# Two transformer layers on one core: the second layer's value products in pairs

## The chip, the core and the metric

The kernel runs on one core of one Trainium2 chip. The metric is device time in microseconds of one execution. The core has the engines that the profile names PE (TensorE, the matrix engine; PEld are its weight loads), DVE (VectorE), ACT (ScalarE), POOL (GpSimd) and SP (SyncE, which here only issues transfers). They work beside each other and wait for one another by semaphores; each takes its instructions in the order in which the program wrote them.

## The reference

The input `x` has 4 batches of 1024 tokens with 128 features, all in float32. Four blocks follow each other, each added to `x` after a layer norm:

```python
x = x + _layernorm(_L0_attn_ref(_layernorm(x), L0_attn_Wqkv, L0_attn_Wout))
x = x + _layernorm(_L0_ffn_ref(_layernorm(x), ...))      # attention and mixture of experts
x = x + _layernorm(_L1_attn_ref(_layernorm(x), L1_attn_w_qkv))
x = x + _layernorm(_L1_ffn_ref(_layernorm(x), U1, V1, b1, U2, V2, b2))
```

Three of these hold a causal attention with 16 heads:

```python
att = jnp.einsum('bhqd,bhkd->bhqk', q, k) * scale     # scores
att = jnp.where(causal, att, -jnp.inf)
att = jax.nn.softmax(att, axis=-1)
out = jnp.einsum('bhqk,bhkd->bhqd', att, v)           # value products
```

In the first and third attention a head has 8 features; the first clips its scores to plus and minus 10. The second attention, inside `_L0_ffn_ref`, takes keys and values from a latent of 16 features that all heads share, with rotary positions on part of the key; a mixture of 8 experts, two for each token, and a shared expert follow it.

## The kernel before

The kernel calls the three attentions its three layers: the classes `First`, `Second` and `Third`. A layer has 4 batches, and each batch 4 units of 4 heads: 48 units in all, numbers 0 to 15, 16 to 31 and 32 to 47. Within a unit there are two blocks of 512 queries (`h` is 0 or 1), and within a block a loop over key tiles of 128 tokens (`kt`): 4 tiles for `h` = 0, 8 for `h` = 1, because the rest is masked out. So a unit has 12 steps, and a layer 192. From tile 4h on a tile crosses the diagonal (the diagonal tiles): only the queries from `q0` on are computed, 512, 384, 256 and 128 of them.

**One step of the second and third layer.** For each of two pairs of heads (`pp` 0 and 1):

- `scores`: two matmuls of keys by queries into `ps_k`, for two heads beside each other in TensorE's rows. The second layer has 64 rows for each head (the profile writes 64\*128), the third 32 (32\*128).
- `weigh`: ACT takes the exponential of the two score tiles into a tile `pt`; on a diagonal tile POOL then masks the corner with an affine select (line 1257). `pt` has six buffers.
- `max_step`: two matmuls of scores the other way round, into `ps_q`, and their row maxima by DVE, for a unit about one unit ahead. The exponentials of both layers need these maxima beforehand: they are written as extra rows of the operands (`strips`), over a transpose (`ps_n`), a copy on ACT (`nT`) and a transfer issued by SP.

The scores of these two layers, the maxima and most other work share a ring of seven PSUM banks; the sum of the value products, `av`, has a bank of its own. Each float32 matmul shows as two instructions, which stream the operand twice.

**The value products.** `products` multiplies one key tile's weights `pt` by the values of four heads: four matmuls beside each other in TensorE's columns (128\*32, eight instructions), added up in `av` over the block's tiles. Two of the four read the `pt` of `pp` 0, and two that of `pp` 1. With a block's last tile `av` is copied to `num` by ACT, and the transposes to tokens (`ps_a`) are put among the other work for one step later.

The products of a tile are not written in the tile's own step. At the end of a step the tile is appended to `waiting`, and `next_products(keep)` takes the oldest entry if more than `keep` are there. It is called at these places:

- first layer and the very last unit: after both pairs' scores, with `keep` = 1;
- second layer (`u.width == R`): after both pairs, with `keep` = 0;
- third layer: between the two pairs, after `max_step` of the first one, with `keep` = 0.

So `waiting` also carries entries over from block to block and from layer to layer.

**Other work.** At the end of each step `other_work` writes pieces of projections, preparations and tails: the second layer's tail holds the experts (`pgu`, `pc`, `py`), the third layer's tail the feed-forward with its activation on 512-wide tiles (`ph` on TensorE, `sq` and `xb` on ACT, lines 1010 and 1011 on POOL). A planner in Python, at build time, chooses the pieces by due times and by an account of the work that TensorE, ACT and DVE still owe (`Metered`, `behind`); value products count in TensorE's account. All matmuls, ACT and DVE operations are recorded in a helper, so they all have line 96, and the profile is read by the names of the tiles.

Of the kernel before, what the change touches and what calls it, by code (L numbers as in the profile page):

```python
# [121 lines left out]
def sandwich(ctx: ExitStack, tc: tile.TileContext, a: dict, out: bass.AP):  # L122
# [20 lines left out]
    def mtile(name):  # L143
        return ring[0].tile([P, 512], F32, tag="s", name=name) if ring else ps_spare.tile([P, 512], F32, tag="m", name=name)
# [371 lines left out]
    def to_tokens(num, dst, width, ps, n=4):  # L516

        for i in range(n):
            nc.tensor.transpose(ps[:, i * P : (i + 1) * P], num[:, i * P : (i + 1) * P], ident)
        ps4 = ps[:, 0 : n * P].rearrange("p (i j r) -> p i j r", i=n, j=4)  # L520
        rec = pool2.tile([P, 4, 4], F32, tag="rec3", name="rec3")[:, 0:n]
        nc.vector.reciprocal(rec, ps4[:, :, :, width])
        nc.vector.tensor_tensor(
            dst.rearrange("p i (j d) -> p i j d", j=4), ps4[:, :, :, 0:width],
            rec.unsqueeze(3).to_broadcast([P, n, 4, width]), ALU.mult,
        )
# [605 lines left out]
    def need_free(k):  # L1132

        while not stages[k].att_free:
            behind[0][1].look(step_now[0])
            behind[0][1].piece(step_now[0])
            if behind[0][1].done:
                behind.popleft()

    def need_prep(n):  # L1140
        for i in range(n + 1):
            if not prep[i].done:
                need_input(i // NG)
                prep[i].finish()
# [19 lines left out]
    def max_step(n, h, qt, c, pp, mx, last):  # L1164
        u, g = units[n]
        need_prep(n)
        if h not in mx:
            mx[h] = pool2.tile([P, 4, 2, 2, h + 1], F32, tag=f"mx{h}", name="mx")
        w = min(512, (qt + 1) * P - 512 * c)
        ps = rtile("ps_q")  # L1170
        for jj in range(2):
            q, k = u.rows(g, pp, jj)
            nc.tensor.matmul(
                ps[jj][:, 0:w], lhsT=q[:, qt * P : (qt + 1) * P], rhs=k[:, 512 * c : 512 * c + w], start=True, stop=True
            )
        for jj in range(2):
            scores, to = ps[jj][:, 0:w], mx[h][:, qt - 4 * h, pp, jj, c : c + 1]
            if c == h:

                nc.vector.tensor_tensor_reduce(  # L1180
                    scores, scores, cmask[:, 512 - w : 512], 1.0, -3.0e38, ALU.add, ALU.max, to
                )
            else:
                nc.vector.tensor_reduce(to, scores, AX.X, ALU.max)
        if last:
            negated[n, h] = Task(u.negate(g, h, mx[h]))
            urgent.append(negated[n, h])

    def after(task, gen):
        yield LIGHT, 2  # L1190
        task.finish()
        yield from gen

    def products(n, h, kt, state, pts, q0):

        u, g = units[n]
        last = 4 * h + 3
        if kt == 0:
            state["acc"] = ps_av.tile([P, 512], F32, tag="av", name="av")
        acc = state["acc"]  # L1200
        for j in range(4):
            nc.tensor.matmul(
                acc[32 * j : 32 * j + 32, q0:512], lhsT=u.values(g, kt, j), rhs=pts[j // 2][:, j % 2, q0:512],
                start=kt == 0, stop=kt == last, tile_position=(0, 32 * j),
            )
        if kt == last:
            num = pool2.tile([P, 512], F32, tag="num", name="num")
            if n == len(units) - 1:

                for i in range(2):  # L1210
                    half = slice(256 * i, 256 * i + 256)
                    nc.scalar.copy(num[:, half], acc[:, half])
                    quarters.append(Task(u.quarter(num, 2 * h + i), 26))
                return
            nc.scalar.copy(num, acc)

            def back():
                yield SPARE, 2
                to_tokens(num, u.result(g, h), u.width, mtile("ps_a"))

            k = n // NG
            if g == 0 and h == 0 and k > 0:
                if u.width == R or stages[k - 1].width == R:
                    need_free(k - 1)
                elif k > 1:
                    need_free(k - 2)
            urgent.append(Task(back()))
            if g == NG - 1 and h == 1:
                tails[k] = Task(after(urgent[-1], u.tail()), u.pieces[1])
                behind.append((24 * NG * (k + 2) - 6, tails[k]))  # L1230

    def scores(n, h, kt, pps):

        u, g = units[n]
        q0 = max(0, kt * P - 512 * h)
        tiles = [rtile("ps_k") if ring else two_banks("ps_k") for pp in pps]
        for pp, ps in zip(pps, tiles):
            for jj in range(2):
                q, k = u.rows(g, pp, jj)
                nc.tensor.matmul(  # L1240
                    (ps[jj] if ring else ps[:, jj])[:, q0:512], lhsT=k[:, kt * P : (kt + 1) * P], rhs=q[:, 512 * h + q0 : 512 * h + 512],
                    start=True, stop=True,
                )
        return tiles, q0

    def weigh(n, h, kt, ps, q0):
        u, g = units[n]
        pt = pool6.tile([P, 2, 512], F32, tag="pt", name="pt")
        if ring:
            for jj in range(2):  # L1250
                nc.scalar.activation(pt[:, jj, q0:512], ps[jj][:, q0:512], AF.Exp, scale=u.scale)
        else:
            nc.scalar.activation(pt[:, :, q0:512], ps[:, :, q0:512], AF.Exp, scale=u.scale)
        u.clip(pt[:, :, q0:512])
        if kt >= 4 * h:

            nc.gpsimd.affine_select(  # L1257
                out=pt[:, :, q0 : q0 + P], in_=pt[:, :, q0 : q0 + P], compare_op=ALU.is_ge, fill=0.0, base=0,
                pattern=[[0, 2], [1, P]], channel_multiplier=-1,
            )  # L1260
        return pt
# [31 lines left out]
    def other_work(at, light=4):  # L1293

        taken = set()
        nc.pass_step()
        while t := pick(at, taken):
            if t.kind == LIGHT:
                light -= 1
                if not light:  # L1300
                    taken.add(LIGHT)
            else:
                taken.add(t.kind)
            t.piece(at)
# [7 lines left out]
    waiting = deque()  # L1312

    def next_products(keep):
        if len(waiting) > keep:
            products(*waiting.popleft())

    at = 0
    for n, (u, g) in enumerate(units):
        if n == B * NG:  # L1320
            first_banks.close()
            ring.append(ctx.enter_context(tc.tile_pool(name="ps_one", bufs=7, space=PSUM)))
        need_prep(n)
        for h in range(2):
            if n == 0 and h == 1:
                u.second.finish()
            if u.has_max and not negated[n, h].done:
                negated[n, h].finish()
            state = {}
            for kt in range(4 * h + 4):  # L1330
                if not u.has_max or n == len(units) - 1:

                    (a0, a1), q0 = scores(n, h, kt, (0, 1))
                    pts = [weigh(n, h, kt, ps, q0) for ps in (a0, a1)]
                    next_products(1)
                    for _ in range(2):
                        at += 1
                        if maxima and maxima[0][0] <= at:
                            max_step(*maxima.popleft()[1])
                else:  # L1340
                    pts = []
                    for pp in range(2):
                        (ps,), q0 = scores(n, h, kt, (pp,))
                        pts.append(weigh(n, h, kt, ps, q0))
                        at += 1
                        if maxima and maxima[0][0] <= at:
                            max_step(*maxima.popleft()[1])
                        if pp == 0 and u.width != R:
                            next_products(0)
                    if u.width == R:  # L1350
                        next_products(0)
                other_work(at)
                waiting.append((n, h, kt, state, pts, q0))
    while waiting:
# [53 lines left out]
```

## Time and profile before

| what | value |
|---|---|
| runs | 2198.24, 2201.5 and 2203.89 us, median 2201.5 |
| profiled execution, from first to last instruction | 2195.8 us |
| TensorE busy | 2102.2 us, 96% |
| DVE, ACT, POOL busy | 66%, 58%, 28% |
| scores `ps_k`, second layer (64\*128) | 1536 instructions, 335.9 us |
| value products `av`, second layer | 1536 instructions, 163.7 us |
| value products `av`, first and third layer | 3072 instructions, 336.9 us |
| masks on the diagonal, POOL line 1257 | 768 instructions, mean 445 ns |

The profiled execution has no time of its own beside its span: 2195.8 us is what its instructions cover, and the runs' median stands 5.7 us above that. Starts are counted from the span's first instruction. In the rows of the timeline an arrow in brackets names what ended the idle time before an instruction; the length of a matmul includes a modelled end, so two matmuls in a row overlap on paper. In a table by stages the columns are the stretch, its length, the busy time of PE, PEld, DVE, ACT and POOL with the number of instructions, the granted share of TensorE's clock, the DMA share and GB/s.

### The profile page before, as it was taken

How to read it: one execution, taken by the hardware profiler on the slowest of the kernel's cores; microseconds unless marked ns; L12 is line 12 of the kernel's file. 1: busy time of each engine (PE TensorE's matmuls, PEld its weight loads, DVE VectorE, ACT ScalarE, POOL GpSimd, SP SyncE). 2: the span in 40 equal slices, each digit the busy share in tenths (PEclk: the TensorE clock that was granted, in tenths of full speed). 3: DMA queues.
4: the chain of work that ended last, by engine and by line, in shares of the span. 5: the costliest groups of instructions: out<-in, count | busy, mean ns of one | idle time of the engine just before them, and what ended most of it. 6: DMA issues, size and time to landing. Idle time of an engine off the chain costs nothing.

```text
span 2195.8 us, 40904 instructions
## 1 busy us (share of the span) xinstructions
PE 2102.2 (96%) x14480; PEld 907.0 (41%) x14480; DVE 1444.6 (66%) x4265; ACT 1279.8 (58%) x2680; POOL 621.6 (28%) x1032
## 2 busy tenths in 40 slices
PE   7999999989999999999999999999999999999994
PEld 2333333324444444444444544343444444444432
DVE  5666666577656675567566675567668677677755
ACT  3676767744555554455445544455556766766776
POOL 3342323432233222223222211221122233322332
PEclk9999999999999999999999999999999999999996
DMA  2310000111111101111020100000000000000000
GB/s 58 66 17 11 11 11 11 26 39 26 26 39 31 26 16 35 26 26 26 6 54 18 26 9 6 7 7 6 7 7 7 12 7 17 12 7 16 7 1 20
DMA packets 32253, 42.98 MB, mean 20 GB/s; under 512 B 11553, under 2 KB 23841, under 8 KB 32049
## 3 DMA queue, kind: packets, MB, share of 16 engines
q1 hardware_dynamic: 31440, 40.04, 8.4%
q8 instruction: 115, 1.88, 0.4%
q14 instruction: 90, 0.73, 0.1%
q10 hardware_dynamic: 608, 0.33, 0.1%
HBM read 5.74 MB, written 2.10 MB: 4 GB/s over the span
## 4 chain that ended last, share of the span: by engine, by line
PE 83%; ACT 6%; DVE 6%; POOL 2%; issue 2%; DMA 0%; SPq 0%; ACTq 0%; POOLq 0%; DVEq 0%
PE ps_k L96 29%; PE ps_q L96 18%; PE av L96 18%; PE pgu L96 3%; ACT pt L96 3%; PE ps_a L96 2%; PE py L96 2%; PE pa L96 2%; DVE pt L96 1%; PE ps_t L96 1%; PE ps_p L96 1%; PE ps_o L96 1%; PE ps_v L96 1%; DVE ps_q L96 1%; PE ps_l L96 1%
## 5 line engine op out<-in xcount | busy, mean ns | idle before, releaser
L96 ACT ACTIVATE pt<-ps_k 128x512 f32<-128x512 f32 (+5 forms) x1920 | 952.0, 555 | 640.3 <-PE ps_k L96 440.8
L1257 POOL TENSOR_SCALAR_AFFINE_SELECT pt<-pt 128x256 f32<-128x256 f32 x768 | 333.5, 445 | 1173.0 <-ACT pt L96 864.7
L96 DVE CUSTOM_DVE_ANT_0 ps_q<-ps_q,cmask 128x256 f32<-128x256 f32 (+3 forms) x1024 | 481.1, 515 | 213.1 <-PE ps_q L96 204.9
L96 PE MATMUL ps_k<-strips 32*128 32x512 f32 (+3 forms) x3072 | 573.0, 538 | 9.7 <-ACT pt L96 2.4
L96 DVE TENSOR_REDUCE mx<-ps_q 128x1 f32<-128x512 f32 x512 | 328.7, 684 | 153.8 <-PE ps_q L96 152.3
L96 PE MATMUL ps_q<-strips 32*128 32x512 f32 (+3 forms) x1536 | 423.9, 537 | 6.0 <-ACT pt L96 3.5
L96 PE MATMUL av<-pt,vals 128*32 128x512 f32 (+3 forms) x3072 | 336.9, 502 | 25.3 <-ACT num L96 11.2
L96 PE MATMUL ps_k<-strips,kT 64*128 64x512 f32 (+3 forms) x1536 | 335.9, 511 | 1.2 <-ACT nT L96 1.2
L96 PEld LDWEIGHTS ps_k<-strips 32*128 32x128 f32 x3072 | 213.5, 186 | 285.4 <-ACT pt L96 105.6
L96 PE MATMUL ps_q<-kT,strips 64*128 64x512 f32 (+3 forms) x1536 | 323.1, 489 | 0.9 <-ACT pt L96 0.6
L96 DVE TENSOR_SCALAR pt<-pt 128x1024 f32<-128x1024 f32 (+3 forms) x384 | 227.1, 607 | 133.9 <-ACT pt L96 129.0
L96 PEld LDWEIGHTS ps_q<-kT,strips 64*128 64x128 f32 x1536 | 152.6, 188 | 117.6 <-issue 69.4
L96 PEld LDWEIGHTS ps_q<-strips 32*128 32x128 f32 x1536 | 164.3, 185 | 73.1 <-ACT pt L96 44.9
L96 PEld LDWEIGHTS ps_k<-strips,kT 64*128 64x128 f32 x1536 | 130.7, 186 | 150.6 <-issue 65.3
L96 PEld LDWEIGHTS av<-pt,vals 128*32 128x32 f32 x3072 | 63.6, 109 | 244.0 <-issue 106.8
L96 PE MATMUL av<-pt,v2l 128*32 128x512 f32 (+3 forms) x1536 | 163.7, 498 | 0.0
L96 DVE DVE_READ_ACCUMULATOR2_ANT mx<- 128x1 f32 x1024 | 144.5, 141 | 0.0
L384 POOL TENSOR_TENSOR rs<-rs,minus_half 128x8 f32<-128x8 f32 (+1 forms) x38 | 62.4, 1643 | 251.3 <-DVE rs L96 250.8
L96 PEld LDWEIGHTS av<-pt,v2l 128*32 128x32 f32 x1536 | 30.3, 108 | 104.6 <-issue 61.8
L96 PEld LDWEIGHTS ps_a<-ident,num 128*128 128x128 f32 x384 | 40.2, 140 | 72.3 <-issue 52.5
L96 PE MATMUL ps_a<-ident,num 128*128 128x128 f32 x384 | 63.3, 287 | 0.4 <-ACT num L96 0.4
L96 ACT COPY num<-av 128x512 f32<-128x512 f32 (+1 forms) x98 | 57.1, 586 | 10.5 <-PE av L96 10.1
(278 smaller groups left out, 1628.2 us busy)
## 6 DMA issues: line engine op xcount, KB each, us to landing
swapped<-rb SPq DMA_DIRECT2D x32, 256.0 KB
strips<-rp SPq DMA_DIRECT2D x64, 128.0 KB
strips<-packed SPq DMA_DIRECT2D x248, 32.0 KB
strips<-lat SPq DMA_DIRECT2D x64, 64.0 KB
strips<-nT SPq DMA_DIRECT2D x256, 1.0 KB
strips<-nT SPq DMA_DIRECT2D x128, 2.0 KB
x<-in_L_attn_x_dram SPq DMA_DIRECT2D x3, 512.0 KB
out_dram<-x SPq DMA_DIRECT2D x3, 512.0 KB
```

Of the source, the lines that this page charges most:

```text
L96: return call(*args, **kw)
L384: nc.gpsimd.tensor_tensor(rs[:, t], rs[:, t], minus_half[:, t], ALU.pow)
L1257: nc.gpsimd.affine_select(out=pt[:, :, q0 : q0 + P], in_=pt[:, :, q0 : q0 + P], compare_op=ALU.is_ge, fill=0.0, base=0, pattern=[[0, 2], [ ...
```

## The change

In the second layer the products are no longer written in each step. `paired_products` writes them when two tiles of the block wait, or when the oldest waiting tile belongs to another block than the current one, and then `next_products(0)` is to take all that wait. For this the `if` in `next_products` becomes a `while`. The other calls of `next_products` are left as they are.

```diff
     def next_products(keep):
-        if len(waiting) > keep:
+        while len(waiting) > keep:
             products(*waiting.popleft())
+
+    def paired_products(n, h):
+        if len(waiting) == 2 or waiting and waiting[0][:2] != (n, h):
+            next_products(0)
...
                         if pp == 0 and u.width != R:
                             next_products(0)
                     if u.width == R:
-                        next_products(0)
+                        paired_products(n, h)
                 other_work(at)
                 waiting.append((n, h, kt, state, pts, q0))
```

## The prediction, made before the changed kernel ran

> **What bounds the kernel now.** I read the page first, then the busy time by stage, then TensorE's timeline inside the second and the third layer.
>
> ```profile
> PE 2102.2 (96%) x14480; PEld 907.0 (41%) x14480; DVE 1444.6 (66%) x4265; ACT 1279.8 (58%) x2680; POOL 621.6 (28%) x1032
> PE 83%; ACT 6%; DVE 6%; POOL 2%; issue 2%; DMA 0%; SPq 0%; ACTq 0%; POOLq 0%; DVEq 0%
> ```
>
> TensorE is busy for 96% of the span, and the chain that ended last runs through it for 83%. The stretches below are the second layer (its first value products start at 528 us) and the third (from 1443 us).
>
> ```profile
> 528.00:1443.00 915.00, 911.97 (x5625) 424.10 (x5624) 575.35 (x1743) 463.34 (x1057) 227.88 (x352) 1.00 0.10 23
> 1443.00:2149.00 706.00, 690.24 (x5128) 293.50 (x5128) 497.16 (x1635) 459.46 (x1083) 194.69 (x332) 0.99 0.05 8
> ```
>
> After the stretch come PE, PEld, DVE, ACT and POOL busy time and the granted clock. In both layers TensorE leaves 1 to 2% free and DVE, ACT and POOL 30% or more. So a microsecond less on TensorE is a microsecond less in all, and a wait put into TensorE's queue is lost.
>
> TensorE in the second layer (start, length, output, shape; x4 is a pair of matmuls in two passes each):
>
> ```profile
> 902.49 1.13 PE L96 MATMUL ps_k<-strips,kT 64*128 64x512 f32 x4
> 903.45 0.60 PE L96 MATMUL ps_q<-kT,strips 64*128 64x256 f32 x4
> 903.88 1.02 PE L96 MATMUL ps_k<-strips,kT 64*128 64x512 f32 x4
> 904.74 0.81 PE L96 MATMUL ps_q<-kT,strips 64*128 64x384 f32 x4
> 905.48 0.64 PE L96 MATMUL av<-pt,v2l 128*32 128x256 f32 x8
> 906.05 1.13 PE L96 MATMUL pgu<-xTe,wg 128*128 128x512 f32 x2
> ...
> 908.72 0.81 PE L96 MATMUL ps_q<-kT,strips 64*128 64x384 f32 x4
> 909.36 0.81 PE L96 MATMUL ps_k<-strips,kT 64*128 64x384 f32 x4
> ```
>
> Lengths include a modelled end, so I go from start to start. The same ps_q group of 384 columns takes 0.74 us when av follows (904.74 to 905.48) and 0.64 when ps_k follows (908.72 to 909.36): a change of shape costs 0.10. The av group takes 0.57 where two passes of 256 columns take 0.43 (the ps_q row at 903.45): 0.03 between its passes and 0.11 on leaving. ps_k after another shape takes 0.96 (902.49), after ps_q 0.86 (903.88): 0.10 more on coming back. A group of value products that stands alone between ps_q and ps_k thus costs 0.10+0.14+0.10 = 0.34 us beyond its passes. If side work of full shape follows, that work pays the return anyway, and the products' own share is 0.24.
>
> **Second layer, shape changes.** It has 16 units of 12 key tiles: 192 groups today, one in each step. Afterwards the 96 odd steps have none, and the even steps have two behind each other. A second group of the same shape behind the first should cost what a second pass does, 0.03 and 0.03 again; no row shows it, and the bounds are 0.02 and, with a full shape change, 0.12. Taking the group out of a step without side work saves 0.34-0.06 = 0.28; out of a step with side work 0.24-0.10-0.06 = 0.08, since ps_q to the side work is then a change itself. In the timeline ps_k follows directly on 32 of the 96 odd-step groups; on 64, side work does. That is 32 x 0.28 + 64 x 0.08 = 14.1 us. One thing moves: a block's last products now run in the first step of the next block and not in the second, so its transposes to tokens (ps_a, due one step later) go from the third step into the second. 23 steps that had only them lose a change (23 x 0.10 = 2.3 back), and 17 odd steps that had no side work get it (17 x 0.30 = 5.1 lost). Shape changes save 14.1+2.3-5.1 = 11.3 us. If the transposes kept their steps it would be 14.1, and with 0.12 in place of the first 0.03 about 3.
>
> **Second layer, waits.** An odd tile's weights are wanted one step sooner. At each slot I compared the end of the first group with the end of the tile's last write (ACT's exponential, or POOL's mask on the diagonal). Of 96 tiles three have under 1.5 us left (-0.05, 0.25, 0.26), all behind POOL side work; the step before, without products, takes 0.85 to 1.1 more away. That is 1.1+0.6+0.6 = 2.4 us lost, so the layer gains 8.9. DVE and ACT could stop TensorE in the faster odd steps, since scores there follow each other without a break; the seven banks hold most of a step's eight score tiles, and the even steps are longer by as much, so I take 0 (bounds 0 and 5). Buffers: two waiting tiles and the current one hold six weight tiles, and the pool has six. No DMA is issued by a moved step; num's copy on ACT comes one step sooner with a whole step more before av is written again.
>
> **Third layer, which the title does not name.** The loop that hands out products turned from `if` into `while`. Before, two entries are left waiting by the first layer, and through the second and the third one is taken for each one added: products lag two steps. The timeline shows it: at 1640.05 the products are 384 columns wide (key tile 5) while the scores are 128 wide (tile 7). Afterwards the queue is emptied at the first slot, and the third layer's products lag one step: tile kt-1 is multiplied after half of the scores of kt. Nothing is saved by that, but less time is left for ACT and POOL:
>
> ```profile
> 1605.64 0.96 POOL L1257 TENSOR_SCALAR_AFFINE_SELECT pt<-pt 128x256 f32<-128x256 f32 x2 [1.66 <-ACT pt L96]
> 1605.80 1.07 PE L96 MATMUL av<-pt,vals 128*32 128x512 f32 x8
> ...
> 1718.37 0.62 POOL L1010 TENSOR_SCALAR sq<-sq 128x512 f32<-128x512 f32 x1
> 1719.07 1.29 POOL L1011 TENSOR_TENSOR sq<-sq,xb 128x512 f32<-128x512 f32 x1
> 1719.58 1.07 PE L96 MATMUL av<-pt,vals 128*32 128x512 f32 x8
> 1720.30 2.43 POOL L1257 TENSOR_SCALAR_AFFINE_SELECT pt<-pt 128x256 f32<-128x256 f32 x4
> ```
>
> At 1605.80 TensorE multiplies tile 0. Afterwards tile 1 stands in this slot, and its mask (the first of the two, 0.41 us) ends at 1606.04: 0.24 late. At 1719.58 it multiplies tile 4; tile 5's two masks stand behind two pairs of POOL steps of the feed-forward tail (0.62 and 1.28 us each) and end at 1722.02: 2.4 late. Read so for all 179 slots of units 32 to 46, tiles below the diagonal have 0.6 us or more. On the diagonal 53 are late: 43 short ones, 6.9 us in sum (tile 1 and tile 5 by 0.24, tile 2 by 0.07, tile 4 by 0.13, some of tile 6 by 0.28), and ten long ones, 24.0 in sum, nine of them behind those tail steps. Where TensorE already waits for a mask, its matmul starts 0.05 behind it (in the first layer); against the slot that is 0.04 more for each, 2.2 in all. Sum 33.1 us. The late mask is local to its tile: ACT and DVE wait for TensorE around it, so it is not made up. Behind the waiting products stand the next scores, and behind these ACT and DVE.
>
> Two terms I can only bound. TensorE waits in the third layer already, about 23 us hidden and open; some of that comes right behind a new wait and would shrink: 0 to 10, I take 4. And the clock: a wait can cost more than its length.
>
> ```profile
> 1449.63 1.22 PE L96 MATMUL ps_k<-strips 32*128 32x512 f32 x2 [1.95 <-DMA strips<-nT]
> 1449.40:1452.70 3.30, 3.07 (x20) 0.79 (x20) 0.91 (x2) 1.58 (x4) 0.00 (x0) 0.50 0.00 0
> ```
>
> After a wait of 1.95 us the granted clock was 0.50 for 3.4 us, which takes 1.7 us of work. Of the six waits of 1.4 us and more between 380 and 1460 us four were followed by this (1.58, 1.95, 2.16, 2.96) and two not (1.45, 1.85). For nine long waits of 2.4 to 2.8 us the bounds are 0 and 9 x 1.7 = 15; I take six, 10 us.
>
> The Trainium skill, "TensorE: Matmul & The Clock Gate", section "Why this matters for your kernels", tells to avoid idle gaps over about 3 us, after which the clock halves. By that these waits would cost nothing extra and the sum would be 10 us lower; the row above, halved after 1.95, speaks against it, and I follow the row.
>
> **Sum.** The third layer loses 33.1-4+10 = 39.1, the second gains 8.9: +30 us. The planner that places side work weighs TensorE's owed time, which the products change by up to 852 ns in a step, so some side work will shift by a step: 5 us either way. The profiled execution's span is 2195.8 and would be 2226; the median of the runs, 2201.5, stands 5.7 above the span (what lies around it, and the spread of 5.7 between runs), so I forecast 2201.5+30 = 2231.
>
> **Rivals.** *Fewer long waits* (0.19): the shifted planner puts most tail steps on POOL beside tiles below the diagonal. Four long ones (9.6), the short ones (6.9+2.2), 4 for the clock, less 2 and 8.9: +12, 2213. For it: slack there is 0.6 us or more; against it: 8 of 12 tiles of a unit are diagonal, and the same pattern stands in units 37, 41 and 45. *Faster* (0.07): ACT or DVE, not TensorE, sets the third layer's pace, so that a wait at the products only takes the place of a later one at the banks. Then the second layer's 9 to 14 us stay: 2190. It decides if the third layer grows by under 2 us; against it are DVE's 70% and ACT's 65% there. *Clock throughout* (0.05): all ten long waits halve the clock and nothing is absorbed, 33.1+15-6 = +42, 2244. *About even* (0.07): the third layer loses what the second gains. That the pairs would not form is excluded: blocks have 4 or 8 tiles, so pairs never straddle.
>
> **How the numbers follow.** The case of +30, with 20 to 40 around it, holds 0.62. A measurement of this kernel tells about 0.3%, 6.6 us, from no change. Faster 0.07, same 0.08 (with the edge of the fewer waits), slower 0.85. The range goes from just under the fewer-waits case to the clock case, 2207 to 2245.
>
> **What would show it.** Right: av groups in pairs of eight plus eight in the second layer with about 0.06 us extra between them, that layer 7 to 14 us shorter; in the third layer new TensorE waits for POOL's masks of some 30 us, nine of about 2.5, and more half-clock time there. Wrong: a third layer that is no longer than before, or a second layer in which TensorE waits for banks.

## The result, and the profile after

The changed kernel takes 2253.1 us (median of 5 runs, 2251.1 to 2257.2) against 2201.5 us before: a ratio of 1.0238, with a 95% interval of 1.0223 to 1.0253. It is 51.6 us slower; 2231 was forecast, with 2245 as the upper end. The profiled execution's span grew by 53.6, from 2195.8 to 2249.4 us.

The page of the changed kernel, busy time and chain:

```profile
PE 2125.5 (94%) x14480; PEld 933.6 (42%) x14480; DVE 1436.1 (64%) x4265; ACT 1279.0 (57%) x2680; POOL 623.6 (28%) x1032
PE 80%; ACT 6%; DVE 5%; POOL 5%; issue 2%; DMA 0%; SPq 0%; ACTq 0%; POOLq 0%; DVEq 0%
```

The instructions are the same in number. TensorE is busy 23 us longer and idle some 30 us longer, and POOL has come into the chain with 5% instead of 2%. By stage, cut at the first exponential of units 16, 32 and 47 (columns as in the first table):

```profile
519.50:1438.30 918.80, 906.80 (x5635) 442.49 (x5631) 567.39 (x1746) 463.10 (x1058) 227.05 (x356) 1.00 0.10 23
1438.30:2173.10 734.80, 699.98 (x4965) 295.58 (x4963) 491.94 (x1602) 438.69 (x1024) 189.26 (x315) 0.95 0.05 8
```

The kernel before, cut in the same way:

```profile
519.90:1437.30 917.40, 914.37 (x5639) 425.33 (x5639) 575.88 (x1746) 464.35 (x1058) 227.65 (x356) 1.00 0.10 23
1437.30:2119.60 682.30, 670.59 (x4966) 287.34 (x4969) 492.80 (x1606) 438.42 (x1025) 186.63 (x315) 0.99 0.05 9
```

The second layer, which the change is named after, is 1.4 us longer; the third is 52.5 longer, and the mean clock granted in it fell from 0.99 to 0.95. The first layer is equal.

TensorE's timeline in the second layer:

```profile
580.87 1.02 PE L96 MATMUL ps_q<-kT,strips 64*128 64x512 f32 x4
581.83 1.71 PE L96 MATMUL av<-pt,v2l 128*32 128x512 f32 x16
583.47 0.49 PE L96 MATMUL ps_k<-strips,kT 64*128 64x128 f32 x4
583.79 1.03 PE L96 MATMUL ps_q<-kT,strips 64*128 64x512 f32 x4
584.65 0.39 PE L96 MATMUL ps_k<-strips,kT 64*128 64x128 f32 x4
584.88 0.39 PE L96 MATMUL ps_q<-kT,strips 64*128 64x128 f32 x4
```

The products come as sixteen instructions, and the price of a shape change is what it was: 0.10 before av, 0.11 after it, and ps_k takes 0.32 us on coming back (583.47) against 0.23 (584.65). From one group's second pass to the next group's first the start-to-start time is 0.430 us for 512 columns, which is the 0.43 that 512 columns took in the prediction's rows: a second group of the same shape adds less than 0.01 us.

The same layer has something else that was not there before:

```profile
772.25 1.65 POOL L384 TENSOR_TENSOR rs<-rs,minus_half 128x8 f32<-128x8 f32 x1
773.94 0.35 DVE L96 TENSOR_TENSOR rs<-rs 128x8 f32<-128x8 f32 x1 [4.87 <-POOL rs L384]
774.21 0.28 DVE L96 CUSTOM_DVE_ANT_0 ps_q<-ps_q,cmask 128x128 f32<-128x128 f32 x1
774.61 0.28 PE L96 MATMUL ps_n<-ident,neg 128*16 128x128 f32 x1 [2.76 <-DVE mx L96]
```

A piece of side work on DVE waits 4.87 us for a root on POOL, which stands behind other POOL work. DVE's row maxima are queued behind that piece, and TensorE, which needs them, stands for 2.76 us. In the kernel before the piece stood elsewhere in the order and waited 0.49 us. The same happens once more four units later (2.38 us), and these two units are 3.2 and 2.9 us longer.

The third layer, at the place that the prediction showed (unit 37, tile 5):

```profile
1726.27 0.62 POOL L1010 TENSOR_SCALAR sq<-sq 128x512 f32<-128x512 f32 x1
1726.97 1.27 POOL L1011 TENSOR_TENSOR sq<-sq,xb 128x512 f32<-128x512 f32 x1
1728.19 2.06 POOL L1257 TENSOR_SCALAR_AFFINE_SELECT pt<-pt 128x256 f32<-128x256 f32 x3
1729.11 2.33 PE L96 MATMUL av<-pt,vals 128*32 128x384 f32 x8 [1.55 <-POOL pt L1257]
1731.37 0.80 PE L96 MATMUL ps_k<-strips 32*128 32x256 f32 x2
```

The products of 384 columns now stand where those of 512 stood, wait for the mask behind the POOL steps, and take 2.26 us (1729.11 to 1731.37) where 0.78 is usual. Two things are in this: the first heads run and the last wait again for the second mask, and the granted clock is 0.5 from 1728.7 on, so that a pass of 384 columns takes 0.64 us there and not 0.32. The two largest TensorE waits of the third layer, with total, number and longest, and one of its stretches at half clock:

```profile
PE av L96 <- POOL pt L1257: 22.9, 14, 2.5
PE ps_q L96 <- ACT pt L96: 3.6, 14, 0.3
```

```profile
1919.90:1933.50 13.60, 12.07 (x67) 5.25 (x64) 4.86 (x21) 7.07 (x17) 5.76 (x9) 0.50 0.00 1
```

The waits view counts only what lies behind a matmul's modelled end. For a full account I took, for each group of products, the time from the end of the columns before it to the first matmul that reads the late mask, less the usual 0.10. In the third layer these come to 36.3 us, against 2.7 before: twelve long ones of 1.5 to 2.9 us behind the tail's POOL steps, and the rest short. The sum depends on how it is counted: with the columns before a group taken at the clock granted there, and up to the heads that read the later mask (they start 0.05 to 0.06 us behind its end), 42 late groups come to 40 us, 30 of them in the long ones, against nothing before. The granted clock is 0.5 for 68.3 us of the layer, against 13.7. I call these two numbers product waits and half-clock time below.

### The profile page after: what moved, and what is told of

The parts are those of the page before. It is cut to its first block, busy times and chain, and to the rows that moved or that the text cites. A ratio compares the mean times of both kernels' runs of the same rounds, so it can differ in the third digit from the quotient of the medians.

```text
span 2249.4 us, 40942 instructions
## 1 busy us (share of the span) xinstructions
PE 2125.5 (94%) x14480; PEld 933.6 (42%) x14480; DVE 1436.1 (64%) x4265; ACT 1279.0 (57%) x2680; POOL 623.6 (28%) x1032
## 4 chain that ended last, share of the span: by engine, by line
PE 80%; ACT 6%; DVE 5%; POOL 5%; issue 2%; DMA 0%; SPq 0%; ACTq 0%; POOLq 0%; DVEq 0%
PE ps_k L96 29%; PE av L96 18%; PE ps_q L96 16%; ACT pt L96 3%; PE pgu L96 3%; PE ps_a L96 2%; PE py L96 2%; PE pa L96 2%; DVE pt L96 1%; POOL sq L1011 1%; PE ps_p L96 1%; PE ps_o L96 1%; PE ps_t L96 1%; PE ps_v L96 1%; PE ps_l L96 1%
## 5 line engine op out<-in xcount | busy, mean ns | idle before, releaser
L96 PE MATMUL ps_k<-strips 32*128 32x512 f32 (+3 forms) x3072 | 581.9, 544 | 12.0 <-DVE mx L96 4.2
L96 PE MATMUL av<-pt,vals 128*32 128x512 f32 (+3 forms) x3072 | 358.2, 511 | 47.0 <-POOL pt L1257 31.7
L96 PEld LDWEIGHTS av<-pt,vals 128*32 128x32 f32 x3072 | 70.0, 109 | 278.1 <-POOL pt L1257 111.1
L96 PE MATMUL av<-pt,v2l 128*32 128x512 f32 (+3 forms) x1536 | 145.3, 492 | 1.2 <-POOL pt L1257 1.2
L96 PEld LDWEIGHTS av<-pt,v2l 128*32 128x32 f32 x1536 | 40.2, 109 | 106.1 <-issue 75.9
```

What stands on the lines that cost most here:

```text
L96: return call(*args, **kw)
```

## The experiments

**Pairs alone.** The third layer gets its lag of two steps back.

```diff
                         if pp == 0 and u.width != R:
-                            next_products(0)
+                            next_products(1)
```

> The second layer's pairs as in the change; the third layer keeps its lag of two steps. Theory A (the third layer loses by the shorter lag, the second gains a little by shape changes and gives it back in two waits behind moved side work): the third layer is as long as before, the second 0 to 3 us longer as in the change: 2198 to 2207 us. Rival B (the pairs shift the side work, and the shift makes the third layer longer): the third layer stays 30 us or more longer, over 2230.

Measured: 2202.8 us, ratio 1.0013 (0.9999 to 1.0027). By stage:

```profile
519.70:1438.70 919.00, 906.87 (x5635) 442.44 (x5631) 567.84 (x1746) 463.39 (x1058) 227.69 (x356) 1.00 0.10 23
1438.70:2128.80 690.10, 678.61 (x4968) 290.03 (x4970) 492.99 (x1606) 439.08 (x1025) 187.54 (x315) 0.98 0.05 9
```

The second layer is as long as in the change, the product waits of the third are 2.3 us, and the slowdown is gone. The profiled execution is one of the longer ones (2206.9 us): its third layer is 7.8 us longer than before, with 34.1 us at half clock against 13.7. What makes the second layer's pairs is not what makes the third layer longer.

**Lag alone.** The second layer's products stay single and two steps behind; the third layer's lag one step.

```diff
                     if u.width == R:
-                        paired_products(n, h)
+                        next_products(1)
```

> The second layer's products singly in each step, two steps behind, as before; the third layer's lag is one step. Theory A: the third layer is some 52 us longer, all else as before: 2248 to 2258 us. Rival B: under 2215.

Measured: 2244.8 us, ratio 1.0190 (1.0169 to 1.0210), 42.6 us more than before and a little under the range. The third layer:

```profile
1435.30:2168.00 732.70, 697.16 (x4963) 295.07 (x4955) 492.27 (x1602) 438.45 (x1025) 188.32 (x315) 0.96 0.05 8
```

The second layer has its old 917.4 us; the third has 732.7, with 36.0 us of product waits and 58.0 us of half-clock time. Most of the loss, 42.6 of 51.6 us, is the lag's. The 8 us between this and the change are only partly found in the profiles: 1.4 in the second layer and 2.1 in the third.

**The tail's two POOL steps on DVE,** in the changed kernel and in the kernel before (lines 1010 and 1011; the planner is charged as before).

```diff
-                        nc.gpsimd.tensor_scalar(sq, sq, 0.044715, 1.0, ALU.mult, ALU.add)
-                        nc.gpsimd.tensor_tensor(sq, sq, xb, ALU.mult)
+                        tc.nc.vector.tensor_scalar(sq, sq, 0.044715, 1.0, ALU.mult, ALU.add)
+                        tc.nc.vector.tensor_tensor(sq, sq, xb, ALU.mult)
```

> The changed kernel with the feed-forward tail's two steps on 128x512 moved from POOL to DVE, the planner's account unchanged. Theory A (the twelve long waits for masks that stand behind these steps, with the half clock that follows them, make most of the loss): only short waits of some 9 us stay, half-clock time in the third layer falls from 68 to about 20 us, 2205 to 2222 us. Rival C (the shorter lag costs in every tile, through the exponentials): over 2240.

> The kernel before with the same two steps on DVE. Theory A: masks are early there, so nothing waits for POOL and nothing is won: within 5 us of 2201.5. Rival D (POOL's load costs time before the change too): 2195 or less.

Measured: 2237.4 us (ratio 1.0153, 1.0132 to 1.0173) and 2218.9 us (1.0074, 1.0052 to 1.0095). Both expectations missed: the move itself costs the kernel before 16.7 us. The third layer with the steps on DVE, changed kernel and kernel before:

```profile
1445.70:2157.20 711.50, 696.95 (x4965) 296.62 (x4963) 513.67 (x1650) 437.19 (x1024) 142.46 (x267) 0.97 0.05 9
1435.40:2139.00 703.60, 693.92 (x4966) 295.48 (x4967) 513.26 (x1654) 438.39 (x1024) 142.28 (x267) 0.96 0.05 9
```

In the kernel before, product waits are 2.6 us, but half-clock time is 58.0 against 13.7. The layer's 21.3 us more lie in TensorE's busy time (693.9 against 670.6 us for the same instructions) and not in waits, so nearly all of them are the lower clock's: 0.48 us for each microsecond at half clock, if all are. What in DVE's fuller queue brings the half clock on was not tested. Between the two kernels with DVE, product waits are 9.6 against 2.6 us: without the POOL steps ahead of the masks the long waits are gone, as expected. What the shorter lag then still costs cannot be read from this pair. The runs are 18.5 us apart and the third layers 7.9, while half-clock time goes the other way, 40.5 against 58.0 us.

**The old lag where the POOL steps stand.**

```diff
                         if pp == 0 and u.width != R:
-                            next_products(0)
+                            next_products(int(h == 1 and n in (37, 38, 41, 42, 45, 46)))
```

> The changed kernel, but in the six blocks of eight tiles of the third layer beside which the feed-forward tail's POOL steps stand (h = 1 of units 37, 38, 41, 42, 45 and 46), the products lag two steps as before; everywhere else one step as in the change. Theory A (long waits for masks behind those POOL steps, and the half clock after them, make some 45 of the 52 us; the short waits 7): 2206 to 2216 us, half-clock time in the third layer 30 us or less. Rival C (the shorter lag costs in every block alike; 52 us over 30 blocks, of which 6 are mended): 2240 or more.

Measured: 2212.6 us, ratio 1.0045 (1.0027 to 1.0063), 9.2 us over the kernel before. Product waits are 14.6 us and half-clock time 27.3. TensorE's waits in the third layer:

```profile
PE av L96 <- POOL pt L1257: 6.1, 5, 1.6
```

Six of 30 blocks carry some four fifths of the loss: 40.6 of 51.6 us. A cost of the shorter lag in every block alike is excluded.

**Fillers in the waits.** Two matmuls that nobody reads ahead of each of the twelve groups that wait long in the changed kernel.

```diff
+    LONG = {(u, 1, k) for v in (37, 41, 45) for u, ks in ((v, (5, 7)), (v + 1, (4, 6))) for k in ks}
...
+        if (n, h, kt) in LONG:
+            spare = mtile("filler")
+            for _ in range(2):
+                tc.nc.tensor.matmul(spare, lhsT=ident, rhs=cmask, start=True, stop=True)
```

> The changed kernel with two matmuls of 128x128 by 512 columns, whose result nobody reads, ahead of the twelve groups of value products that wait 1.5 to 2.9 us for POOL in the third layer; they take about 1.8 us of TensorE where it would have waited. Theory A1 (of the third layer's 52 us about 20 are the half clock that the waits bring on): half-clock time there falls from 68 us to 30 or less and the time to 2230 to 2242 us. Rival E (the waits themselves are the loss, and the half clock costs little since TensorE has room in it): 2250 to 2260 us, whatever the clock does.

Measured: 2237.9 us, ratio 1.0169 (1.0147 to 1.0192): 15.2 us faster than the change, with more work in it. The place shown above, with the filler (line 1263 is line 1257 of the other kernels):

```profile
1726.79 0.62 POOL L1010 TENSOR_SCALAR sq<-sq 128x512 f32<-128x512 f32 x1
1727.49 1.27 POOL L1011 TENSOR_TENSOR sq<-sq,xb 128x512 f32<-128x512 f32 x1
1728.01 1.98 PE L1202 MATMUL filler<-cmask,ident 128*128 128x512 f32 x4
1728.72 2.05 POOL L1263 TENSOR_SCALAR_AFFINE_SELECT pt<-pt 128x256 f32<-128x256 f32 x3
1729.93 1.38 PE L96 MATMUL av<-pt,vals 128*32 128x384 f32 x8
1731.24 0.48 PE L96 MATMUL ps_k<-strips 32*128 32x256 f32 x2
```

And the third layer:

```profile
1439.70:2157.80 718.10, 702.88 (x5013) 298.56 (x5011) 491.94 (x1602) 438.38 (x1025) 189.34 (x315) 0.99 0.05 9
```

TensorE works where it stood, the clock stays full at this place, and ps_k follows the waiting products 1.31 us after their start instead of 2.26. A filler takes 1.91 us, twelve take 23; product waits fall by 21.6 us to 14.7, so these two about cancel. Half-clock time falls by 51.2 us to 17.1 and the third layer by 16.7 to 718.1: about 0.33 us for each microsecond at half clock, if the two cancel.

**The same fillers in the kernel before,** ahead of the same groups, where TensorE does not wait.

> The kernel before with the same fillers ahead of the same twelve groups of products, where TensorE does not wait: each of the twelve costs its two matmuls, about 1.9 us. Theory A1 (a microsecond put into TensorE's queue in the third layer is lost, whatever else happens): 22 us more, 2219 to 2228 us. Rival I (TensorE has slack in these blocks): under 2212 us.

Measured: 2220.1 us, ratio 1.0077 (1.0060 to 1.0094), 16.8 us more, in the range at its lower edge. Where I compared single steps, two of the fillers cost some 1.26 us each of their 1.91: a bank wait just behind had been 0.65 long. So most of what is put into TensorE's queue is lost, but not all.

**Products after both pairs.** The changed kernel with the third layer's products half a step later.

```diff
-                        if pp == 0 and u.width != R:
-                            next_products(0)
                     if u.width == R:
                         paired_products(n, h)
+                    else:
+                        next_products(0)
```

> The changed kernel, but the third layer's products stand after both pairs' scores and maxima, half a step (0.4 to 1.1 us of TensorE) later; the lag is one step as in the change. Theory A (local waits for late masks): the short waits vanish, the twelve long ones shrink to about 1.3 us each, half-clock time falls with them: 2212 to 2232 us. Rival C (the shorter lag costs by itself): 2245 or more.

Measured: 2270.9 us, ratio 1.0309 (1.0282 to 1.0336). A miss in the total, though the step it was made for did what was expected: product waits are 3.0 us. TensorE's waits in the third layer:

```profile
PE ps_q L96 <- ACT pt L96: 13.1, 29, 1.6
PE ps_k L96 <- ACT sq L96: 9.3, 12, 1.1
```

In the kernel before these were 3.5 and 1.5 us. With no products between the two pairs the four groups of scores follow each other, and TensorE runs into the seven banks that ACT has not emptied; half-clock time is 88.7 us. The products between the pairs had also been spacing.

**Pairs, with the side work left in place.** The second layer's pairs, the third layer's lag of two steps, the planner charged for single products, and the transposes to tokens kept in their step.

```diff
+    def as_if_single(write):
+        owed = nc.owed["PE"]
+        write()
+        nc.owed["PE"] = owed
+        if shadow:
+            nc.owed["PE"] += 0.833 * 2 * (512 - shadow.popleft())
...
-                            next_products(0)
+                            next_products(1)
+                            shadow.popleft()
...
-                        paired_products(n, h)
+                        as_if_single(lambda: paired_products(n, h))
...
+                shadow.append(q0)
...
-                yield SPARE, 2
+                yield SPARE, 4 if (15, 1) <= (n, h) < (31, 1) else 2
```

`shadow` holds the first query column of each tile, so that the account is charged for the tile that would have been due.

> The second layer's pairs with the third layer's lag of two steps, the planner's account of TensorE charged as if the products stood singly in each step, and the transposes to tokens kept in their step, so that the side work stays nearly where it was before. Theory F (shape changes save 10 to 16 us, and the moved side work gave most of it back): second layer 10 to 15 us shorter than before, 2187 to 2195 us. Rival G (shape changes save only about 5 us): 2196 to 2202 us.

Measured: 2195.6 us (9 runs, 2191.3 to 2202.0), ratio 0.9974 (0.9961 to 0.9987), at the edge between the two expectations. It is the only version faster than the kernel before. The second layer:

```profile
519.40:1428.90 909.50, 902.74 (x5635) 443.58 (x5631) 572.42 (x1746) 462.82 (x1058) 226.80 (x356) 1.00 0.10 24
```

It is 7.9 us shorter than before and 9.3 shorter than in the change, and the two long waits for DVE are gone. Steps with the same side work in both kernels can be compared, less their products' passes. Odd steps without side work are 0.24 us shorter (median), and where no wait comes between, the even step behind them gains another 0.06 to 0.10 at its first scores. Odd steps with side work are 0.14 shorter. Of 19 whose only side work is the transpose of the maxima, the seven at a unit's end are 0.14 shorter too; eleven of the other twelve, all a unit's fourth step, are 0.05 to 0.47 longer, most of them because the scores behind the transpose wait 0.2 to 0.6 us for DVE's row maxima. An even step with both groups is 0.01 longer. Some of TensorE's waits in the second layer, in the kernel before and then here:

```profile
PE ps_o L96 <- ACT attT L96: 0.9, 3, 0.3
```

```profile
PE ps_o L96 <- ACT attT L96: 2.5, 6, 0.6
PE ps_k L96 <- DVE mx L96: 1.5, 5, 0.5
```

Counted from the end of the columns before and less the usual 0.10, all of TensorE's waits in the layer rise from 4.7 to 9.5 us.

**Pairs in both layers.** As the last one (the diff is against it), with the third layer's products in pairs too, after both pairs' scores, and its transposes to tokens kept in their step as well.

```diff
...
-                        if pp == 0 and u.width != R:
-                            next_products(1)
-                            shadow.popleft()
-                    if u.width == R:
-                        as_if_single(lambda: paired_products(n, h))
+                    as_if_single(lambda: paired_products(n, h))
```

> As the pairs with the planner's account kept, and the third layer's products in pairs as well, after both pairs' scores in every second step. Theory F: the third layer saves as many shape changes, 10 to 20 us, less the waits of odd diagonal tiles behind the tail's POOL steps (three to six of about 1.3 us): 2172 to 2192 us. Rival H (in steps without products the banks or ACT hold the scores back, or the clock falls): over 2200 us.

Measured: 2253.9 us, ratio 1.0239 (1.0218 to 1.0259). The third layer has 741.9 us. Product waits are 2.7 us, but the waits at the banks for ACT are there as with products after both pairs (12.8 and 10.5 us), and half-clock time is 92.2 us.

## Why the prediction was wrong

**Right.** TensorE set the end, so its waits were lost, or most of them. The `while` shortened the third layer's lag, and that, not the pairs, decided the sign: lag alone costs 42.6 us, pairs alone 0.6. The waits for masks were sized well: 33.1 us predicted; measured 36.3 - 2.7 = 33.6 by one count and 40 by the other, with twelve long ones for the ten that were read. They stood where the prediction put them, behind the tail's POOL steps, as the old lag in six blocks showed. That the first count meets the prediction so closely is partly luck.

In the profiles the loss is 53.6 us where +30 was forecast. Of the 23.4 us between, 13.4 are in the third layer (52.5 against 39.1) and 10.3 in the second (1.4 lost against 8.9 gained).

**The clock, priced at 10 us with at most 15.** This term failed in the third layer. I let each long wait bring one stretch of 3.4 us, six in all. The stretches came as 3.4, 6.8, 10.2 and 13.7 us: 54.6 us more at half clock, where six stretches would have been 20. For the price of one microsecond the runs give 0.33 (the fillers), 0.38 (pairs alone, 7.8 us longer with 20.4 more at half clock) and 0.48 (the kernel before with the POOL steps on DVE), where I had taken one half. That makes some 18 to 26 us. Nor do long waits alone set the clock: that last kernel has 58.0 us at half clock almost without product waits, so a count of long waits could not give the term. The Trainium skill, "TensorE: Matmul & The Clock Gate", "Part 1: The HAM clock gate", has the busy clock return after a busy window of about 3.4 us; here it stayed at 0.50 for 13.6 us in which TensorE was busy for 12.1, so that is not enough of a rule for these matmuls. Whether this is because they fill only a part of the array was not tested.

**The absorption, taken as 4 us.** Waits of 33.6 to 40 us and 18 to 26 of clock make 52 to 66, against 52.5 measured. So it may be nothing or more than 4; the runs do not separate it. The filler in the kernel before shows that it exists at single places.

**The second layer, +8.9 us predicted, 1.4 lost.** Two parts. The shape changes were priced from rows that held: 0.10, 0.11 and 0.10, 0.34 in all where no wait comes between, and the second group cost 0.01 instead of 0.06. What failed is the term that was put at 0, that DVE and ACT could stop TensorE in the faster odd steps. Even with the side work in place TensorE's waits rise by 4.8 us, and the layer gains 7.9, not the 14.1 less 2.4 that the prediction had for transposes that keep their step. And the shift of the side work, for which I had named 5 us either way and put nothing into the sum, cost: two units are 6.1 us longer together, through DVE waiting for POOL. With the planner charged as before they are 1.6 longer. Some of the 9.3 us between the two orders may be the transposes' step, which was changed together with the charge.

**The range** ended at 2245 because the clock's upper bound was too low and because no case had the second layer losing while the third did.

## What to carry to other kernels

A loop that takes one entry from a queue and a loop that empties it differ for everyone who uses the queue afterwards: look for entries that are left over from an earlier stage, because they are a lag that later stages live on. Before a lag is shortened, compare in the timeline, slot by slot, when the operand is ready and when it will be read; what stands ahead of the operand on its engine sets the wait, and the sum of that count was right here to within a fifth. A wait on a busy TensorE has to be priced with the clock that it may lose, and where a planner places work by an account, a change to the account is a change of its own that should be tried by itself.

## What the runs showed of the hardware

- Half clock on a busy TensorE: in the change the granted clock fell to 0.50 beside waits of 1.5 to 2.9 us and stayed there for up to 13.7 us, and two matmuls put into each of the twelve long waits took 51.2 of the 68.3 us away. But waits are not needed for it. In pairs alone it lasted 23.9 us with TensorE busy throughout (first line), with no wait of TensorE over 0.15 us in the 6.9 us before; in the kernel before with the POOL steps on DVE it did so too (second line). What sets it there stays open.

```profile
1496.80:1520.70 23.90, 23.90 (x121) 9.88 (x120) 15.53 (x50) 8.95 (x22) 3.27 (x5) 0.50 0.07 10
1494.80:1518.70 23.90, 23.90 (x121) 9.73 (x120) 15.53 (x50) 8.93 (x22) 3.26 (x5) 0.50 0.07 11
```

- The same kernel's runs differ with it: nine runs of the pairs with the side work in place lie between 2191.3 us at a mean clock of 0.983 and 2202.0 at 0.974.
- A change of TensorE's tile shape costs 0.10 to 0.11 us on either side, and the first scores after it another 0.10; groups of one shape behind each other cost less than 0.01. The Trainium skill, "TensorEngine Tiling (Array Packing)", section "Tiling Modes", says that a change of mode drains the engine; the rows above show what a change costs, but not that the drain is its cause.
